# A two-layer graph network on one core: the order of the setup on VectorE, the schedule of the last blocks, and where the test's result is kept

## The chip, the core and the metric

The kernel runs on one core of a Trainium2 chip. The core has five engines with their own instruction streams: TensorE (PE; its weight loads are listed as PEld), VectorE (DVE), ScalarE (ACT), GpSimd (POOL) and SyncE (SP). DMAs are issued from the streams of SP and ACT, and gathers by index from POOL. The metric is the device time of one execution in microseconds (us), as the median of several. Beside it stands one profiled execution, whose span runs from the first to the last instruction.

## The reference

There are 12,500 nodes with 256 features each (`x`) and 200,000 edges (`src`, `dst`), sorted by `dst`. The draw makes `dst` go with the square of the edge's place: edge e of E points to about node 12500 (e/E)^2, so early nodes have many edges and late nodes few.

```python
def _sage_conv(x, src, dst, W_l, b_l, W_r):
    msgs = x[src]
    agg = jax.ops.segment_sum(msgs, dst, num_segments=N_NODES)
    deg = jax.ops.segment_sum(jnp.ones((src.shape[0],), x.dtype), dst, num_segments=N_NODES)
    mean = agg / jnp.maximum(deg, 1.0)[:, None]
    return mean @ W_l + b_l + x @ W_r
h = jax.nn.relu(_sage_conv(x, src, dst, W1_l, b1, W1_r))
h = jax.nn.relu(_sage_conv(h, src, dst, W2_l, b2, W2_r))
out = layernorm(x + h @ W3 + b3)
```

## The kernel before

**Two ways of summing.** Edges are cut into 1,563 tiles of 128, nodes into 98 blocks of 128. The first nodes, which have most edges, are summed as dense products: seven groups of 256 nodes, five of them in layer 1. For each group the kernel counts how many edges lead from every node to each of the 256 (`count`, L678 and below: comparisons `pick`, `low` and `aft` on DVE, products on PE, the result copied into `counts`), and then multiplies the table of all rows, split into three bf16 parts, with these counts (`product`, L667). Layer 2 uses the counts of layer 1 again: four are stored in DRAM and loaded, and one group is kept. The other nodes are summed by gathering: four indirect DMAs on POOL (L257) fetch 512 rows of a round into one of four buffers `got`; PE adds up 32 neighbouring nodes per tile (`part_ps`, L269), ACT copies the result (`some`), PE moves it to its place (`sum_ps`, L285), and DVE adds it to a ring of eight blocks, `sums` (L299).

**Blocks.** When a block's sums are complete, `first_block` (layer 1, in three pieces) or `last_block` (layer 2, in five) turns its own rows over on PE (L861), forms the products with the two weights (L884, L889), adds and applies the relu. The last layer turns h over again, forms the product with W3 (L956), and takes the layernorm on DVE and ACT. Layer 1 writes h to `h_d`, and its three parts to `h3_d`; both are read by layer 2, and a profile writes both as h_d.

**The order.** On PE and POOL the order is the program's own (`manual_schedule`, L445). The rounds of gathers set it: `layer` (L584) runs round after round, and in three parts of each round it places one piece of a waiting block, and as much of the counting and dense work (`dense`, a generator) as is due by then. The amount due grows evenly, from estimated costs, and reaches the whole 8 rounds before the last. A block waits in line from the round in which its sums are complete by the law of the draw: `at_least(t)` and `at_most(t)` bound the node that tile t begins with, by the square law moved by `SLACK` = 8 tiles. After the last round the rest of the dense generator is run out, and then the blocks that wait. The dense generator puts its two blocks in line only when it is run past its last product. With the amounts of this program, layer 2 reaches this point after the loop: blocks 6 and 7, of the last dense group, stand at the very end.

On DVE, ACT and SP a planner orders the instructions by its own simulated times and by the program's order as priority. Within an engine instructions then run in the order written, each waiting for its semaphores. A DMA of SP or ACT uses one of eight semaphores, and in the trace it waits until the DMA that used the semaphore before has landed.

**The setup.** `src` and `dst` are loaded as 13 x 128 x 128 integers by SP (`edges`, L304): `src_i`, `dst_i` and `nxt_i`, which is `dst` one edge on. ACT loads the first `dst` of tiles: of each tile by fours (`f4_i`, L333 and L337), by eights (`f8_i`, L340), of all early tiles (`f1_i`, L342), `fours_i` and `pair_i` (L343, L345). Indices are cast to floats, turned over on PE with the identity `ident` (L361), and written by DVE into tables (`columns`, L376): `src_t` (the gathers' indices), `lo_t` (an edge's place within its tile's 32 nodes), `lo2` (L433, a tile's place within 128). These are what the first gathers need. Behind them come the tables for counting (`low_t`, and `key_t` and `after_t` by group), with a round of gathers started between the groups (`early_round`), and then tests that the drawn edges obey the law and fit into the rooms (L497 to L544), each of which adds to a column of `bad`. The memory of the setup is then reused: ACT blanks the two `counts` there (L574).

**The result of the tests.** After layer 2, PE sums `bad`, DVE reduces it to one flag, and SP writes it to DRAM (L988), reads it back into the chip (L41), and every engine loads it into a register and branches over `by_sorting`, a slower version that fits any edges.

Of the kernel before, what the change touches and what calls it, by code (L numbers as in the profile page):

```python
# [23 lines left out]
P = 128  # L24
# [3 lines left out]
def kernel(tc, x, src, dst, w1l, b1, w1r, w2l, b2, w2r, w3, b3, out):  # L28

    args = (x, src, dst, w1l, b1, w1r, w2l, b2, w2r, w3, b3, out)
    flag = tc.nc.dram_tensor("unfit_d", (1, 1), I32).ap()
    by_runs(tc, *args, flag)
    with tc.tile_pool(name="flag", bufs=1) as pool:
        unfit_i = pool.tile([1, 1], I32, name="unfit_i")  # L40
        tc.nc.sync.dma_start(unfit_i, flag)  # L41
        unfit = tc.nc.values_load(
            unfit_i[0:1, 0:1], min_val=0, max_val=1,
            skip_runtime_bounds_check_because="it is clamped to 0..1 where it is made")
    with tc.If(unfit > 0):
        by_sorting(tc, *args)
# [3 lines left out]
def by_runs(  # L50
# [36 lines left out]
    FAR = 1 << 20  # L87
    SLACK = 8
    RB = 8
    RN = RB * P  # L90
    assert D % P == 0 and E % 2 == 0 and G * W == P


    def at_least(t):
        return N * (max(t - SLACK, 0) / NT) ** 2 - 2

    def at_most(t):
        return N * ((t + SLACK) / NT) ** 2 + 2

# [201 lines left out]
    with tc.tile_pool(name="setup", bufs=1) as su, \  # L301
            tc.tile_pool(name="setup_ps", bufs=2, space=PSUM) as su_ps:
        def edges(a, first, name, fill):
# [14 lines left out]
            return t  # L318

        src_i = edges(src, 0, "src_i", 0)  # L320
        dst_i = edges(dst, 0, "dst_i", FAR)
# [9 lines left out]
        whole = (NT // G) * G  # L331
        with nc.allow_non_contiguous_dma(reason="one edge of each tile"):
            nc.scalar.dma_start(f4_i[:, :NT // G], dst[0:whole * P].rearrange(  # L333
                "(g j l) -> j g l", j=G, l=P)[:, :, 0])
            if NT > whole:
                left = NT - whole
                nc.scalar.dma_start(  # L337
                    f4_i[0:left, NT // G:NG],
                    dst[whole * P:whole * P + (left - 1) * P + 1:P][:, None])
            nc.scalar.dma_start(f8_i, dst[lows[HG1] * P:PAIRS * P].rearrange(  # L340
                "(g j l) -> j g l", j=G, l=2 * P)[:, :, 0])
            nc.scalar.dma_start(f1_i, dst[None, 0:HC * P * P:P])  # L342
            nc.scalar.dma_start(fours_i, dst[0:P * P:P * G][:, None, None].to_broadcast([P // G, G, 1]))  # L343
            for c in range(C0, PAIRS // P):
                nc.scalar.dma_start(pair_i[:, c:c + 1], dst[c * P * P:(c + 1) * P * P:2 * P][  # L345
                    :, None, None].to_broadcast([P // 2, 2, 1]))

# [15 lines left out]
        nc.vector.tensor_copy(lanes_5[:, :, :LW // 5], steps_f[:, :LW].rearrange("p (a b) -> p a b", a=5))  # L363
        nc.vector.tensor_copy(steps_7[:, :, :NB // 7], steps_f[:, :NB].rearrange("p (a b) -> p a b", a=7))


# [65 lines left out]
        nc.vector.tensor_copy(within_f, within)  # L432
        nc.vector.tensor_scalar(lo2, after, within_f, None, op0=OP.add)  # L433

        for g in got:

            nc.vector.memset(g[:, :, D:D + 1], 1.0)
        nc.vector.memset(sums, 0.0)
        nc.vector.memset(degs, 0.0)
        nc.vector.memset(ones, 1.0)  # L440
        nc.vector.memset(ones_b, 1.0)
        nc.vector.memset(zeros_b, 0.0)

# [13 lines left out]

        nc.vector.tensor_copy(steps, steps_f)
        bits = su.tile([P, HC, P], I32, name="bits")
        low = su.tile([P, HC, P], F32, name="low")  # L460
        nc.vector.tensor_scalar(bits, src_i[:, :HC], P - 1, None, op0=OP.bitwise_and)
        nc.vector.tensor_copy(low, bits)
# [4 lines left out]
        start = su.tile([P, HC], F32, name="start")  # L467
        nc.vector.tensor_copy(start[:, 0:1], fours_i)
        nc.vector.tensor_copy(start[:, 1:], first[:, 1:HC])
        f1 = su.tile([1, HC * P], F32, name="f1")  # L470
        nc.vector.tensor_copy(f1, f1_i)
        off_f = su.tile([1, HC * P], F32, name="off_f")
        nxt_first = su.tile([P, HC], F32, name="nxt_first")
        nc.vector.tensor_copy(nxt_first, nxt_i[:, :HC, P - 1])
        most_c = max(b - a for a, b in spans)
# [20 lines left out]
        nxt_f = su.tile([P, CH, P], F32, name="nxt_f")  # L496
        nc.vector.tensor_copy(nxt_f, nxt_i)  # L497
        nc.vector.scalar_tensor_tensor(scr, dst_f, 0.0, nxt_f, op0=OP.add, op1=OP.is_gt,
# [10 lines left out]
        for sign in (-1, 1):  # L509
            law = su.tile([1, NG], F32, name="law", bufs=2)  # L510
            nc.vector.tensor_scalar(law, fours, float(G) / NT, float(sign * SLACK) / NT,
                                    op0=OP.mult, op1=OP.add)
            nc.vector.tensor_scalar(law, law, 0.0, None, op0=OP.max)
            nc.vector.tensor_tensor(law, law, law, op=OP.mult)
            scr4 = su.tile([1, NG], F32, name="scr4", bufs=2)
            nc.vector.tensor_scalar(scr4, f4[0:1], -float(sign), None, op0=OP.add)
            nc.vector.scalar_tensor_tensor(scr4, law, float(N), scr4, op0=OP.mult,
                                           op1=OP.is_gt if sign < 0 else OP.is_lt,
                                           accum_out=test(1))
# [63 lines left out]

    def layer(gathers, block, n_pieces, dense, dense_cost):  # L584

# [35 lines left out]
        for i in range(i0, n + 1):  # L621
            before = gathers.step()
            due = dense_cost * min(1.0, (i + 1 - i0) / (n - i0 - 8))
            for part in range(3):
# [12 lines left out]
    def exact(t, s, rest):  # L637
# [4 lines left out]

        nc.vector.tensor_tensor(rest, t, upper(t), op=OP.subtract)
        nc.vector.tensor_tensor(s[:, 2], rest, upper(rest), op=OP.subtract)
        nc.scalar.copy(s[:, 0], upper(t))
        nc.scalar.copy(s[:, 1], upper(rest))

    def split_rows(b):
        t = load_rows(x, N, b, "split_sb")
        s = work.tile([P, 3, D], BF16, name="parts")  # L650
        exact(t, s, work.tile([P, D], F32, name="rest", tag="own"))
        nc.sync.dma_start(x3_d[:, b], s)
# [320 lines left out]
    with tc.tile_pool(name="count_ps", bufs=2, space=PSUM) as count_pool:  # L973
        layer(gathers_1, first_block, 3, staged(stages_1), cost_of(stages_1))
    block_pool = ctx.enter_context(tc.tile_pool(name="block_ps", bufs=2, space=PSUM))
    count_pool = ctx.enter_context(tc.tile_pool(name="count_ps", bufs=1, space=PSUM))
    w2l_sb, w2r_sb = weight(w2l, "w2l_sb", "wl", nc.sync), weight(w2r, "w2r_sb", "wr", nc.sync)
    layer(Gathers(h_d, True), last_block, 5, staged(stages_2), cost_of(stages_2))


    with tc.tile_pool(name="result", bufs=1) as su:
# [6 lines left out]
        nc.sync.dma_start(flag, unfit)  # L988

# [368 lines left out]
```

## Time and profile before

| | us |
|---|---|
| median of three runs | 2829.16 |
| the three runs | 2829.16, 2819.84, 2829.44 |
| profiled execution, in all | 2817.42 |
| its span | 2815.6 |
| mean granted TensorE clock | 0.928 |
| first gather starts | 26.85 |
| last DVE work of the setup ends | 95.7 |
| last gather of layer 1, first of layer 2 | 1475.51, 1501.29 |
| last gather starts | 2759.22 |
| last product on PE ends | 2799.9 |

Lines of the profile give a start or a total in us, then the engine, the line of the program, the operation, what it writes and reads, its shape, how often it ran, and in brackets how long the engine had been idle before it and what ended that. SPq and ACTq are the moments in which SP and ACT issue a DMA. A group's "idle before" with "issue" is time in which the engine waited for nothing that the profile shows. Digits are left out of tiles' names, so f_i stands for f1_i, f4_i and f8_i, lo for lo2, and h_d for both tables.

### The profile page before, as it was taken

How to read it: one execution, taken by the hardware profiler on the slowest of the kernel's cores; microseconds unless marked ns; L12 is line 12 of the kernel's file. 1: busy time of each engine (PE TensorE's matmuls, PEld its weight loads, DVE VectorE, ACT ScalarE, POOL GpSimd, SP SyncE). 2: the span in 40 equal slices, each digit the busy share in tenths (PEclk: the TensorE clock that was granted, in tenths of full speed). 3: DMA queues.
4: the chain of work that ended last, by engine and by line, in shares of the span. 5: the costliest groups of instructions: out<-in, count | busy, mean ns of one | idle time of the engine just before them, and what ended most of it. 6: DMA issues, size and time to landing. Idle time of an engine off the chain costs nothing. (4 is left out here: it accounts for less than half of the span.)

```text
span 2815.6 us, 54531 instructions
## 1 busy us (share of the span) xinstructions
PE 2321.8 (82%) x18268; PEld 1594.5 (57%) x18268; DVE 1525.3 (54%) x5362; ACT 1098.5 (39%) x2270; POOL 2014.5 (72%) x2074
## 2 busy tenths in 40 slices
PE   3466668988988999999985787778788889999995
PEld 1122225656656766767753565556566666677773
DVE  5688886755655676676662134443233344444443
ACT  0433675655554565565551123342111122222222
POOL 5767677777777777777775777777777767777771
PEclk9977778999989999999999999999899999999997
DMA  4467679869859879868855777777889889888872
GB/s 115 137 202 221 191 219 306 265 193 315 272 183 329 268 234 305 266 194 268 263 167 167 233 249 223 225 228 251 273 282 302 286 282 303 284 264 271 270 241 65
DMA packets 420983, 676.56 MB, mean 240 GB/s; under 512 B 72419, under 2 KB 279385, under 8 KB 420697
## 3 DMA queue, kind: packets, MB, share of 16 engines
q1 hardware_dynamic: 316807, 401.13, 43.7%
q0 software_dynamic: 99072, 270.66, 31.2%
q8 instruction: 150, 2.46, 0.4%
q10 hardware_dynamic: 4818, 1.19, 0.3%
q14 instruction: 136, 1.11, 0.1%
HBM read 582.84 MB, written 89.92 MB: 239 GB/s over the span
## 5 line engine op out<-in xcount | busy, mean ns | idle before, releaser
L257 POOL DMA_INDIRECT got<-in_x_dram,src_t x1076 | 1072.4, 997 | 401.3 <-issue 281.5
L257 POOL DMA_INDIRECT got<-h_d,src_t x988 | 940.0, 951 | 343.7 <-issue 258.7
L667 PE MATMUL dense_ps<-counts,rows 128*128 128x256 bf16 x7056 | 954.0, 278 | 93.6 <-DMA rows<-h_d 53.2
L667 PEld LDWEIGHTS <-rows 128*128 128x128 bf16 x7056 | 671.2, 99 | 316.9 <-issue 84.2
L735 ACT CAST counts<-count_ps 128x686 f32 (+2 forms) x620 | 539.8, 871 | 246.7 <-PE count_ps L729 188.0
L269 PE MATMUL part_ps<-got,one 128*32 128x257 f32 (+1 forms) x4128 | 362.8, 425 | 161.7 <-DMA got<-h_d,src_t 107.6
L729 PE MATMUL count_ps<-pick,low 128*128 128x490 bf16 (+2 forms) x1052 | 320.8, 358 | 57.7 <-DVE low L694 32.0
L691 DVE TENSOR_SCALAR pick<-steps,key_t 128x686 bf16<-128x686 f16 (+2 forms) x748 | 301.1, 405 | 57.6 <-PE count_ps L729 43.0
L213 DVE TENSOR_TENSOR one<-lo_t,lane_b 128x128 f32<-128x128 bf16 x516 | 147.3, 285 | 313.7 <-PE part_ps L269 310.4
L279 ACT COPY some<-part_ps 128x257 f32<-128x257 f32 (+1 forms) x361 | 134.3, 372 | 421.6 <-PE part_ps L269 420.8
L694 DVE TENSOR_SCALAR low<-lanes,low_t 128x130 bf16<-128x130 f16 x748 | 201.7, 271 | 93.7 <-PE count_ps L733 91.9
L269 PEld LDWEIGHTS part_ps<-got,one 128*32 128x32 f32 x4128 | 86.9, 112 | 275.5 <-issue 219.9
L285 PE MATMUL sum_ps<-two,some 128*128 128x128 f32 x1444 | 239.9, 292 | 2.0 <-DVE sums L299 1.9
L892 ACT COPY sums<-zero 128x256 f32<-128x256 f32 x172 | 69.4, 403 | 412.1 <-PE block_ps L889 410.2
L299 DVE TENSOR_TENSOR sums<-sums,sum_ps 128x256 f32 x361 | 148.3, 411 | 145.4 <-PE sum_ps L285 112.7
L285 PEld LDWEIGHTS sum_ps<-two,some 128*128 128x128 f32 x1444 | 208.7, 204 | 16.6 <-issue 9.1
L729 PEld LDWEIGHTS <-low 128*128 128x128 bf16 x1052 | 104.3, 100 | 159.4 <-DVE low L694 61.5
L895 DVE TENSOR_TENSOR own<-block_ps,biases 128x256 f32<-128x256 f32 x196 | 82.7, 422 | 191.7 <-PE block_ps L889 188.4
L863 ACT COPY own_t<-block_ps 128x256 f32<-128x256 f32 x294 | 108.9, 372 | 128.4 <-PE block_ps L861 127.2
L699 DVE TENSOR_SCALAR aft<-steps,after_t 128x98 bf16<-128x98 f16 x621 | 155.9, 251 | 0.0
L898 ACT ACTIVATE h<-own 128x256 f32<-128x256 f32 x196 | 81.6, 416 | 149.6 <-DVE own L896 146.7
L733 PE MATMUL count_ps<-aft,low 128*128 128x98 bf16 x614 | 133.7, 218 | 0.0
(179 smaller groups left out, 2454.6 us busy)
## 6 DMA issues: line engine op xcount, KB each, us to landing
rows<-h_d SPq DMA_DIRECT2D x343, 384.0 KB
rows<-x_d SPq DMA_DIRECT2D x245, 384.0 KB
count_d<-counts SPq DMA_DIRECT2D x28, 896.0 KB
counts<-count_d SPq DMA_DIRECT2D x28, 896.0 KB
x_sb<-in_x_dram SPq DMA_DIRECT2D x194, 128.0 KB
x_d<-parts SPq DMA_DIRECT2D x98, 192.0 KB
h_d<-parts SPq DMA_DIRECT2D x98, 192.0 KB
got<-in_x_dram,src_t POOLq DMA_INDIRECT x1076
```

Of the source, the lines that this page charges most:

```text
L213: nc.vector.tensor_tensor(one, lo[:, a:a + n * (G - 1) + 1:n].unsqueeze(2).to_broadcast([P, G, W]), lane_b[:, :W].unsqueeze(1).to_broadcas ...
L257: rows = nc.gpsimd.indirect_dma_start(out=g[:, j, :D], out_offset=None, in_=self.table, in_offset=bass.IndirectOffsetOnAxis(ap=src_t[:, e: ...
L269: strip = nc.tensor.matmul(part_ps[j * W:(j + 1) * W, :width], lhsT=one[:, j], rhs=g[:, j, :width], start=r == 0, stop=r == n - 1)
L279: nc.scalar.copy(some[:, :width], part_ps[:, :width])
L285: nc.tensor.matmul(sum_ps[:, c], lhsT=some[:, c * P:(c + 1) * P], rhs=two, start=True, stop=True)
L299: nc.vector.tensor_add(own, own, sum_ps[:, :NC])
L667: nc.tensor.matmul(ps[:, c], lhsT=rows[:, b % 2, k, c * P:(c + 1) * P], rhs=c_sb[:, b, :DN], start=False, stop=b == NB - 1 and k == 2 and ...
L691: nc.vector.tensor_scalar(r[:, :w * NB], steps[:, :w * NB], key_t[g][:, t - lo_g:t - lo_g + 1], None, op0=OP.is_equal)
L694: nc.vector.tensor_scalar(low.rearrange("p (a b) -> p a b", a=5), lanes_5[:, :, :LW // 5], low_t[:, t:t + 1], None, op0=OP.is_equal)
L699: nc.vector.tensor_scalar(aft.rearrange("p (a b) -> p a b", a=7), steps_7[:, :, :NB // 7], after_t[g][:, t - lo_g:t - lo_g + 1], None, op0 ...
L729: nc.tensor.matmul(c[:, a * NB:b * NB], lhsT=s, rhs=r[:, a * NB:b * NB], start=True, stop=alone)
L735: nc.scalar.copy(to[:, :, bass.ds(off_act.at(t), w)], c.rearrange("p (d s) -> p s d", s=NB))
```

## The change

Five things change.

- In the setup, DVE is put under the program's order from the first load to `lo2`. The memsets of gather buffers, sums and constants move up, behind the first constants. The six `pair_i` loads move from the end of ACT's loads to their head.
- What comes behind `lo2` on DVE and does not need it in any case gets a dependency on it (`later`): the first instructions of counting, of the tests, and of the first three blocks of split rows.
- The slack of the law is 8 tiles up to tile NT - 65, then 5, and 3 for the last 16. The test of the law (L511) runs over three ranges for each sign, and so has four more instructions.
- `layer` takes the number of rounds by which the dense work ends ahead of the last round, 8 for layer 1 and 14 for layer 2. From there on everything that is left of it is due at once, its last step included.
- The flag is a tile on the chip that lives through the whole program. It is computed between the layers instead of behind layer 2, and neither written to DRAM nor read back.

```diff
-    flag = tc.nc.dram_tensor("unfit_d", (1, 1), I32).ap()
-    by_runs(tc, *args, flag)
     with tc.tile_pool(name="flag", bufs=1) as pool:
-        unfit_i = pool.tile([1, 1], I32, name="unfit_i")
-        tc.nc.sync.dma_start(unfit_i, flag)
+        flag = pool.tile([1, 1], I32, name="flag")
+        by_runs(tc, *args, flag)
         unfit = tc.nc.values_load(
-            unfit_i[0:1, 0:1], min_val=0, max_val=1,
+            flag[0:1, 0:1], min_val=0, max_val=1,
...
-    SLACK = 8
+    SLACKS = [(0, 8), (NT - 64, 5), (NT - 16, 3)]
+    def slack(t):
+        return [by for since, by in SLACKS if since <= t][-1]
     def at_least(t):
-        return N * (max(t - SLACK, 0) / NT) ** 2 - 2
+        return N * (max(t - slack(t), 0) / NT) ** 2 - 2
...
+        in_order = ExitStack()
+        in_order.enter_context(tc.manual_schedule(engines={DVE}))
         src_i = edges(src, 0, "src_i", 0)
...
+            for c in range(C0, PAIRS // P):
+                nc.scalar.dma_start(pair_i[:, c:c + 1], dst[c * P * P:(c + 1) * P * P:2 * P][
+                    :, None, None].to_broadcast([P // 2, 2, 1]))
             nc.scalar.dma_start(f4_i[:, :NT // G], dst[0:whole * P].rearrange(
...
-            for c in range(C0, PAIRS // P):
-                nc.scalar.dma_start(pair_i[:, c:c + 1], dst[c * P * P:(c + 1) * P * P:2 * P][
-                    :, None, None].to_broadcast([P // 2, 2, 1]))
...
+        for g in got:
+            nc.vector.memset(g[:, :, D:D + 1], 1.0)
+        nc.vector.memset(sums, 0.0)
+        nc.vector.memset(degs, 0.0)
+        nc.vector.memset(ones, 1.0)
+        nc.vector.memset(ones_b, 1.0)
+        nc.vector.memset(zeros_b, 0.0)
...
-        nc.vector.tensor_scalar(lo2, after, within_f, None, op0=OP.add)
-        for g in got:
-            nc.vector.memset(g[:, :, D:D + 1], 1.0)
-        nc.vector.memset(sums, 0.0)
...
+        first_tables = nc.vector.tensor_scalar(lo2, after, within_f, None, op0=OP.add)
+        in_order.close()
+        def later(op):
+            tc.add_manual_dep(op.ins, first_tables.ins.name, LANDED, reason="the first gathers' tables")
...
-        nc.vector.tensor_copy(steps, steps_f)
+        later(nc.vector.tensor_copy(steps, steps_f))
...
-        nc.vector.tensor_scalar(bits, src_i[:, :HC], P - 1, None, op0=OP.bitwise_and)
+        later(nc.vector.tensor_scalar(bits, src_i[:, :HC], P - 1, None, op0=OP.bitwise_and))
...
-            nc.vector.tensor_scalar(law, fours, float(G) / NT, float(sign * SLACK) / NT,
-                                    op0=OP.mult, op1=OP.add)
+            for since, by in SLACKS:
+                c = -(-since // G)
+                later(nc.vector.tensor_scalar(law[:, c:], fours[:, c:], float(G) / NT,
+                                              float(sign * by) / NT, op0=OP.mult, op1=OP.add))
...
-    def layer(gathers, block, n_pieces, dense, dense_cost):
+    def layer(gathers, block, n_pieces, dense, dense_cost, left):
...
-            due = dense_cost * min(1.0, (i + 1 - i0) / (n - i0 - 8))
+            due = dense_cost * (i + 1 - i0) / (n - i0 - left) if i + 1 < n - left else 1e8
...
-        exact(t, s, work.tile([P, D], F32, name="rest", tag="own"))
+        leaves = exact(t, s, work.tile([P, D], F32, name="rest", tag="own"))
+        if b < 3:
+            later(leaves)
...
-        layer(gathers_1, first_block, 3, staged(stages_1), cost_of(stages_1))
+        layer(gathers_1, first_block, 3, staged(stages_1), cost_of(stages_1), 8)
...
-    layer(Gathers(h_d, True), last_block, 5, staged(stages_2), cost_of(stages_2))
...
-        unfit = su.tile([1, 1], I32, name="unfit")
-        nc.vector.tensor_scalar(unfit, n_bad, 1.0, None, op0=OP.min)
-        nc.sync.dma_start(flag, unfit)
+        nc.vector.tensor_scalar(flag, n_bad, 1.0, None, op0=OP.min)
+    layer(Gathers(h_d, True), last_block, 5, staged(stages_2), cost_of(stages_2), 14)
```

`later` also stands around the casts of `fours_i`, `f1_i`, `nxt_i` (its last edges and the whole).

More of the change, by code (lines that the diff above doesn't have):

```diff
@@ L91, in by_runs @@
     assert D % P == 0 and E % 2 == 0 and G * W == P
+    def slack(t):
+        return [by for since, by in SLACKS if since <= t][-1]
     def at_least(t):
-        return N * (max(t - SLACK, 0) / NT) ** 2 - 2
+        return N * (max(t - slack(t), 0) / NT) ** 2 - 2
     def at_most(t):
-        return N * ((t + SLACK) / NT) ** 2 + 2
+        return N * ((t + slack(t)) / NT) ** 2 + 2
     HG1, HG, DN = 5, 7, 256
@@ L432, in by_runs @@
         nc.vector.tensor_copy(within_f, within)
-        nc.vector.tensor_scalar(lo2, after, within_f, None, op0=OP.add)
-        for g in got:
-            nc.vector.memset(g[:, :, D:D + 1], 1.0)
-        nc.vector.memset(sums, 0.0)
[L439 to L442, printed above, removed]
+        first_tables = nc.vector.tensor_scalar(lo2, after, within_f, None, op0=OP.add)
+        in_order.close()
+        def later(op):
+            tc.add_manual_dep(op.ins, first_tables.ins.name, LANDED, reason="the first gathers' tables")
         ctx.enter_context(tc.manual_schedule(engines={PE, POOL}))
@@ L467, in by_runs @@
         start = su.tile([P, HC], F32, name="start")
-        nc.vector.tensor_copy(start[:, 0:1], fours_i)
+        later(nc.vector.tensor_copy(start[:, 0:1], fours_i))
         nc.vector.tensor_copy(start[:, 1:], first[:, 1:HC])
         f1 = su.tile([1, HC * P], F32, name="f1")
-        nc.vector.tensor_copy(f1, f1_i)
+        later(nc.vector.tensor_copy(f1, f1_i))
         off_f = su.tile([1, HC * P], F32, name="off_f")
         nxt_first = su.tile([P, HC], F32, name="nxt_first")
-        nc.vector.tensor_copy(nxt_first, nxt_i[:, :HC, P - 1])
+        later(nc.vector.tensor_copy(nxt_first, nxt_i[:, :HC, P - 1]))
         most_c = max(b - a for a, b in spans)
@@ L496, in by_runs @@
         nxt_f = su.tile([P, CH, P], F32, name="nxt_f")
-        nc.vector.tensor_copy(nxt_f, nxt_i)
+        later(nc.vector.tensor_copy(nxt_f, nxt_i))
         nc.vector.scalar_tensor_tensor(scr, dst_f, 0.0, nxt_f, op0=OP.add, op1=OP.is_gt,
@@ L641, in upper @@
             return a.bitcast(BF16).rearrange("p (n h) -> p n h", h=2)[:, :, 1]
-        nc.vector.tensor_tensor(rest, t, upper(t), op=OP.subtract)
+        leaves = nc.vector.tensor_tensor(rest, t, upper(t), op=OP.subtract)
         nc.vector.tensor_tensor(s[:, 2], rest, upper(rest), op=OP.subtract)
@@ L646, in exact @@
         nc.scalar.copy(s[:, 1], upper(rest))
+        return leaves
     def split_rows(b):
```

## The prediction

> **What bounds the kernel now.** I read the busy shares first, then the largest groups, then who held up the gathers, and last three stretches in order of time: the start, the end, and the busiest part of layer 2. First the engines, then the gathers' two groups (busy time, mean of one, idle before them).
>
> ```profile
> PE 2321.8 (82%) x18268; PEld 1594.5 (57%) x18268; DVE 1525.3 (54%) x5362; ACT 1098.5 (39%) x2270; POOL 2014.5 (72%) x2074
> ```
>
> ```profile
> L257 POOL DMA_INDIRECT got<-in_x_dram,src_t x1076 | 1072.4, 997 | 401.3 <-issue 281.5
> L257 POOL DMA_INDIRECT got<-h_d,src_t x988 | 940.0, 951 | 343.7 <-issue 258.7
> ```
>
> PE has the larger share, but POOL sets the pace: an undisturbed gather takes 0.95 us and 0.30 us to issue, so 2064 of them need 2064 x 1.25 = 2580 of the span's 2815.6 us. What POOL waited for (us, times, longest):
>
> ```profile
> POOL got L257 <- issue: 540.1, 1772, 0.6
> POOL got L257 <- PE part_ps L269: 84.5, 69, 9.7
> POOL got L257 <- DMA h_d<-parts: 24.8, 1, 24.8
> POOL got L257 <- DVE src_t L376: 24.1, 1, 24.1
> ```
>
> Besides its own issue, POOL loses 84.5 us to PE in small pieces, 24.8 us once between the layers, and 24.1 us at the start. After its last gather (2760.2) another 55 us pass. So three places can shorten the run: before the first gather, between the layers, behind the last gather. A microsecond saved before the first gather moves all later rounds with it, as long as PE keeps up.
>
> **The setup: about 13 us.** DVE in the order of time, before the change (start, duration, instruction, idle before it):
>
> ```profile
> 10.22 0.83 DVE L382 CAST src_f<-src_i 128x1280 f32<-128x1280 int32 x1 [4.20 <-DMA src_i<-in_src_dram]
> 17.99 0.35 DVE L409 CAST f<-f_i 4x391 f32<-4x391 int32 x1 [6.95 <-DMA f_i<-in_dst_dram]
> ...
> 19.21 0.20 DVE L361 TENSOR_SCALAR ident<-diff 128x128 f32<-128x128 int32 x1
> ...
> 23.99 0.17 DVE L390 CAST begin<-pair_i 128x6 f32<-128x6 int32 x1 [4.44 <-DMA w1l_sb<-in_L_gnn_W_l_dram]
> ...
> 25.88 1.28 DVE L376 TENSOR_SCALAR src_t<-src_ps 128x512 int32<-128x512 f32 x2
> ...
> 36.91 0.40 DVE L433 TENSOR_SCALAR lo<-after,within_f 128x186 f32<-128x186 f32 x1
> ```
>
> The sources are ready as floats at 11.05, but DVE then stands 6.95 us before f4 and 4.44 us before the pairs, with ident (which every transpose needs) and the first eviction of src_t queued behind. The first gather starts at 26.85. In program order ident, lanes and the memsets (sums 1.98, degs 1.02, the rest small) are done by about 8 us, below src's landing. From 11.05: four transposes at 1.97/8 = 0.25 us, 1.0; one eviction, 1.28/2 = 0.64; 0.3 to issue: the first gather starts at about 13, some 14 us sooner.
>
> The rest must follow, or the four gather buffers run full. Four rounds of gathers take 16 x 1.3 = 21 us, so the first part_ps is wanted by 34. On ACT's queue the six pair loads now go first, f4, its rest, f8, f1 and fours behind them. Before, the six took 7.85 us from first to last, most of it waiting for earlier landings; six issues alone are 6 x 0.6 = 3.6. On SP's queue dst_i was issued at 9.12, 6.5 us late behind src_i's landing. I let dst_i land at about 13 (before: 18.8) and f4 and f8 by 19. Then dst_f 1.0, first and begin 0.6, rel 1.5, scr 0.8 and 1.5, transposes and three evictions 3, lo2's part 1.3, the small f4 and f8 work with its two matmuls 5: first tables at about 27, against 37.3. From that 10 comes off what now stands behind them but was done before: steps, two bits, low, high, 0.60 + 0.42 + 0.48 + 0.47 + 0.49 = 2.5 us. DVE was idle for 17 of the 58 us between the tables and the last test (95.6), waiting for gathers that now also come 14 us sooner; 41.5 busy + 2.5 + four more law pieces, 1 us, fit into the stretch. So the end of setup, and with it ACT's 22 us of blanking the counts (95.76 to 117.77) and the first counting, come about 14 us sooner. The stretch 118 to 180, where POOL loses 20 us because counting sets the pace (DVE busy 51.4 of 62), keeps its length and moves too.
>
> A rule that speaks against this: the Trainium skill, "SBUF — State Buffer", section "SBUF: two separate sides", says that a VectorE instruction in a two-port mode shuts GpSimd out and stops the descriptors of its DMAs. Early gathers now lie beside more setup casts. The row: gathers 1 to 40 took 57.2 us instead of 40 x 1.25 = 50, so 7 us are lost already, single gathers 2.36 and 2.67 us. By the row alone nothing is added, since the same instructions meet other gathers; by the rule up to 9 casts and evictions of some 0.8 us, 7 us more, meet gathers that once came after them. I take 1 us, near the row. Setup: 13; ends 7 (dst_i or f8 land where they did) and 17.
>
> **Between the layers: 3 us.** The order of blocks follows from the slack: with 5 and then 3 tiles in place of 8, blocks 88 to 95 become ready one round sooner. In layer 1 block 95's products (L884 and L889, 3.55 us at 1487.04) now stand ahead of the last sum_ps instead of behind it. The two dense blocks of layer 1 were already done seven rounds earlier, so nothing else moves. The last h still waits for deg_d's round trip, 1486.93 to 1494, in which SP held two loads behind an x_sb load until 1490.84; that block's transposes come about 5 us sooner, the row's own landing does not. Between 1 and 5, I take 3. The test's matmul and its two DVE instructions (0.21, 0.15, 0.12) go into this gap and cost nothing; without the gap 0.5.
>
> **Behind the last gather: 16.5 us.** PE's last 40 us:
>
> ```profile
> 2763.38 1.08 PE L269 MATMUL part_ps<-got,one 128*32 128x256 f32 x8 [1.25 <-DMA got<-h_d,src_t]
> ...
> 2772.27 1.06 PE L285 MATMUL sum_ps<-two,some 128*128 128x128 f32 x4
> ...
> 2787.65 1.03 PE L884 MATMUL block_ps<-w2l_sb,d_sb 128*128 128x256 f32 x4
> ...
> 2793.01 1.03 PE L884 MATMUL block_ps<-w2l_sb,d_sb 128*128 128x256 f32 x4
> ...
> 2797.80 2.08 PE L956 MATMUL block_ps<-w_sb,own_t 128*128 128x256 f32 x4 [0.52 <-ACT own_t L863]
> ```
>
> Products of d_sb are blocks 6 and 7 of the last dense group. Its last dense product ends at 2736.6 and d_sb is copied at once, but in PE's written order these blocks are queued only after the loop. Now all dense work is forced out 14 rounds before the end, and blocks 6 and 7 run in rounds 232 to 237, where the four dense steps of a round (4 x 0.83 = 3.3 us) are gone. After the last sum there remain: block 95's transpose and final product; two transposes; the products of 96 and 97 (2 x 2.0); two transposes; two final products. With DVE and ACT between (0.42 + 0.48 + 0.42 + 0.37 and waits) that is 13 us, against 2799.9 - 2772.3 = 27.6. The last sum itself comes 2 us sooner, block 94's products being out of the last round. 14.5 + 2 = 16.5, between 13 and 19.
>
> **The result on chip: 1 us.** SP's last issues:
>
> ```profile
> 2800.94 0.24 SPq L988 DMA_DIRECT2D unfit_d<-unfit  x1
> 2802.15 0.33 SPq L969 DMA_DIRECT2D out_dram<-z  x1
> 2802.95 0.24 SPq L41 DMA_DIRECT2D unfit_i<-unfit_d  x1
> ```
>
> [...] In the trace they landed after 1.09 and 1.12 us, and out's landing (2803.66) comes only 0.4 us before the flag's (2804.07); every engine waited for both before it branched. So by the row 0.4, plus 0.5 for a register load that may come earlier. If the engines no longer wait for out before they branch, the 3.6 us of PE's branch and POOL's 4.15 us drain run ahead, up to 5. I take 1.
>
> **What it costs: 3 us.** In layer 2 the dense work is spread over 233 rounds instead of 239, 2.6% more in each. The busy part (stretch, length, busy time by engine, clock, DMA share, GB/s):
>
> ```profile
> 2400.00:2736.00 336.00, 318.98 (x2570) 243.14 (x2570) 155.39 (x468) 82.98 (x233) 252.80 (x266) 0.99 0.83 268
> ```
>
> POOL is full here (266 x 1.25 = 332), PE at 95%; 2.6% of its dense half is some 4 us, into 17 idle. From 2000 to 2400 PE waits for rows at a DMA share of 0.88 and POOL loses 16 us; 2.6% of that stretch's dense time, 400 x 0.6 x 0.026, is 6. Between 0 and 10, I take 3.
>
> Sum: 13 + 3 + 16.5 + 1 - 3 = 30.5. The profiled execution took 2817.4 us in all (span 2815.6 and 1.8 around it) and would take 2787. It is one of four times of this program, 2817.4, 2819.8, 2829.2 and 2829.4; I subtract from their mean, 2824, and get 2793.5, rounded 2794.
>
> **The rivals.** (1) The early gathers outrun their tables: f8 and f4 land late behind the pairs, or the DVE chain of keys sets the pace. Against it: 17 us of idle DVE. Setup then gives 0 to 2: gain 18, 2806. (2) PE or the row loads bound all of layer 2: then dense work ends no sooner in time, and six rounds are added behind it, 6 x 5 = 30 us, so 2821. For it: rows waits of 46.9 us between 2000 and 2736; against: 1501 to 2000, where PE is busy 77%. (3) Slower: SP, DVE and ACT of the rest are ordered by a planner from its own timing, and a changed start reorders them. The place is SP's queue in layer 2, where a row load stands behind an x_sb load that waits for its buffer, as the deg loads did at 1490.84. It must cost 30.5 us to cancel the gain, and 44 to be slower by 0.5%: rows waits would have to double, 0.13 us on each of 343 loads; then 2840. (4) That the fallback runs: excluded, since the drawn dst stay within 8 nodes of the law over the last 64 tiles, and three tiles there are 48 nodes.
>
> **How the numbers follow.** The forecast 0.68 (2782 to 2806 alone), rival 1 0.15, rival 2 0.10, rival 3 0.07. 0.5% is 14 us, about what a measurement here can tell from no change: below 2815 is faster. Faster 0.66 + 0.13 + 0.03 = 0.82; same 0.02 + 0.02 + 0.07 = 0.11; slower 0.07. Leaving out rival 3 and most of rival 2 above, and a tail below, gives 2779 to 2815.
>
> **What would show it.** First gather near 13 and lo2 near 27 in the timeline; counts blanked from about 82; POOL's wait for h_d near 22; no d_sb products behind the last gather, and 39 us instead of 55 from it to the end; POOL's waits on part_ps in layer 2 up by no more than 10. Wrong it is if first tables come after 35, or if rows waits grow by tens of us.

## The result and the profile after

The changed kernel takes 2788.66 us (median of four, 2780.44 to 2801.16) beside 2829.06 us for the kernel before (four, 2819.84 to 2829.44). The ratio is 0.9873, with a 95% interval from 0.9841 to 0.9905: 36 us faster, between 27 and 45. Measured again later on another chip it was 0.9851 (0.9820 to 0.9883). The forecast of 2794 lies 5 us from the median. Its parts did not all come out as written, and errors of opposite sign stand behind the agreement.

The profiled execution took 2801.16 us (span 2799.4) and is the slowest of its four. The two profiles therefore differ by only 16 us, and one place in layer 2, shown under "The places over ten profiles", has a share in that. First, what POOL waited for (us in all, times, longest):

```profile
POOL got L259 <- issue: 540.7, 1773, 0.6
POOL got L259 <- PE part_ps L271: 110.1, 80, 7.8
POOL got L259 <- DMA h_d<-parts: 24.4, 1, 24.4
...
POOL got L259 <- DVE src_t L390: 8.5, 1, 8.5
```

The wait at the start fell from 24.1 to 8.5 us. The wait between the layers hardly moved (24.8 to 24.4), and waits on part_ps rose from 84.5 to 110.1. Part of the rise is seen in the setup, another in layer 2 (below). POOL's first gather, and DVE in the order of time:

```profile
11.32 1.10 POOL L259 DMA_INDIRECT got<-in_x_dram,src_t  x1 [8.53 <-DVE src_t L390]
```

```profile
4.01 0.21 DVE L366 TENSOR_SCALAR ident<-diff 128x128 f32<-128x128 int32 x1
...
8.39 0.75 DVE L396 CAST src_f<-src_i 128x1280 f32<-128x1280 int32 x1
...
10.35 0.69 DVE L390 TENSOR_SCALAR src_t<-src_ps 128x512 int32<-128x512 f32 x1 [1.21 <-PE src_ps L387]
...
22.54 1.03 DVE L400 CAST dst_f<-dst_i 128x1664 f32<-128x1664 int32 x1 [10.29 <-DMA dst_i<-in_dst_dram]
...
36.11 0.41 DVE L447 TENSOR_SCALAR lo<-after,within_f 128x186 f32<-128x186 f32 x1 [1.35 <-PE after L442]
```

The identity is ready at 4.2 and the first gather starts at 11.32, against 26.85 before. But then DVE, now bound to the program's order, stands idle for 10.29 us in front of dst_f, and lo2 ends at 36.5, no earlier than before (37.3). SP's queue shows why:

```profile
6.17 0.40 SPq L311 DMA_DIRECT2D dst_i<-in_dst_dram  x1
6.94 0.38 SPq L315 DMA_DIRECT2D dst_i<-in_dst_dram  x1
17.64 0.22 SPq L319 DMA_DIRECT2D dst_i<-in_dst_dram  x1
17.91 0.39 SPq L311 DMA_DIRECT2D nxt_i<-in_dst_dram  x1
```

`edges` loads dst_i in three pieces. The two large ones landed by 15.2. The third, one row of 64 integers (L319), was not issued before 17.64: its semaphore was the one that ACT's load of f4 had used, and in the trace f4's last piece landed at 17.63. The small load landed at 22.52, 4.9 us after its issue, and dst_f followed. The profile of before has the same late third piece:

```profile
17.54 0.22 SPq L317 DMA_DIRECT2D dst_i<-in_dst_dram  x1
```

There the DMA that had used its semaphore was the first piece of dst_i itself, which landed at 17.52; the third landed at 18.77. Still the end of the setup came sooner, as ACT's blanking of the counts shows, first before and then after the change:

```profile
95.76 22.01 ACT L574 COPY counts<-zero 128x13034 f32<-128x13034 f32 x2 [8.25 <-DVE scr L544]
```

```profile
84.84 22.01 ACT L587 COPY counts<-zero 128x13034 f32<-128x13034 f32 x2 [3.04 <-DVE scr L557]
```

The end of PE's work:

```profile
2773.07 0.64 PE L271 MATMUL part_ps<-got,one 128*32 128x256 f32 x8
...
2778.17 0.61 PE L287 MATMUL sum_ps<-two,some 128*128 128x128 f32 x4
...
2783.23 1.03 PE L901 MATMUL block_ps<-w2l_sb,sums 128*128 128x256 f32 x4
...
2788.68 1.89 PE L973 MATMUL block_ps<-w_sb,own_t 128*128 128x256 f32 x8
```

No product of d_sb is left here; the last one starts at 2729.5. From the last sum to the last product 12 us pass, where it was 28. SP's only late issues are those of the output:

```profile
2792.19 1.01 SPq L986 DMA_DIRECT2D out_dram<-z  x2
```

The flag is no longer written and read back, and the engines do not come to the branch together any more. In the kernel before all five loaded the flag between 2804.4 and 2804.6. Here PE loads it at 2789.36, while its last products still run, and branches for 3.87 us; ACT loads it at 2791.91, DVE at 2792.43, SP at 2793.25; and POOL's drain of 4.15 us is over by 2775.84, where before it ran from 2810.63 to 2814.78.

### The profile page after: what moved, and what is told of

Read it like the earlier page. It is cut to its first block, busy times and chain, and to the rows that moved or that the text cites. A ratio compares the mean times of both kernels' runs of the same rounds, so it can differ in the third digit from the quotient of the medians.

```text
span 2799.4 us, 54469 instructions
## 1 busy us (share of the span) xinstructions
PE 2322.7 (83%) x18268; PEld 1595.9 (57%) x18268; DVE 1526.5 (55%) x5366; ACT 1099.7 (39%) x2270; POOL 2018.4 (72%) x2074
## 4 chain that ended last, share of the span: by engine, by line
PE 44%; DMA 24%; POOL 12%; issue 8%; DVE 7%; ACT 3%; DVEq 1%; SPq 0%; ACTq 0%; POOLq 0%
PE dense_ps L684 16%; POOL got L259 12%; PE part_ps L271 6%; DMA got<-h_d,src_t 5%; DMA rows<-x_d 5%; PE block_ps L901 5%; PE count_ps L746 4%; PE block_ps L906 4%; DMA rows<-h_d 4%; PE sum_ps L287 4%; DMA x_sb<-in_x_dram 3%; DMA got<-in_x_dram,src_t 2%; PE block_ps L973 2%; DMA x_d<-parts 2%; PE block_ps L878 2%
```

## The experiments

Twelve runs were made, in three groups. The kernel before ran beside each group on the same chip. In the first group that chip was slower: the kernel before took 3318.63 us there. The gathers themselves took as long as elsewhere, but POOL waited far more for PE. In the changed kernel on this chip (us in all, times, longest):

```profile
POOL got L259 <- PE part_ps L271: 288.4, 124, 11.9
POOL got L259 <- remote: 170.9, 103, 3.2
```

"Remote" is a releaser that the trace does not show. So of this group I use the ratios and what happens before the first gather and behind the last. PE's products took no longer there (the median dense product 0.27 us on both chips); what delayed the releases stays open.

**The whole change again (e4, e9).** No edit.

> The changed kernel once more, for a second profile and more times. Theory: the difference to before is near 35 us, the first gather starts near 11 and lo2 ends near 36 again; what the gathers lost between 640 and 880 of layer 1 in the first profile of it is variation between executions and comes out otherwise here. Rival: the loss of about 12 us in these rounds is the change's own and stands here too.

On the slower chip the ratio was 0.9900 (0.9862 to 0.9937), 33 us of 3319. The first gather came at 11.33 again.

> The changed kernel again, beside the runs that follow. Theory: 34 to 40 us faster than before (ratio 0.986 to 0.988); by places 10 before gather 256, 2 between the layers, 16 from the last gather to the last product, 7 from there to the end, less some 4 in layer 2. On a chip of the slower pace the ratio is near 0.99 and the last two places stay.

On a chip on which the kernel before takes 2826.24, the ratio was 0.9851 (0.9820 to 0.9883): 42 us, 33 to 51. The stretch from gather 640 to gather 880, in which the first two profiles differed by 12 us (315.9 and 327.8), took 319.8 here and 323.9 in a second profile of the kernel before. It was a difference between executions, not of the change.

**The setup alone (e1, e11).** The kernel before, with the setup's part of the diff, a slack of 8 everywhere, dense work due as before, and the flag in DRAM:

```diff
+    SLACKS = [(0, 8)]
...
+        in_order.enter_context(tc.manual_schedule(engines={DVE}))
...
+            for c in range(C0, PAIRS // P):
+                nc.scalar.dma_start(pair_i[:, c:c + 1], dst[c * P * P:(c + 1) * P * P:2 * P][
...
+        first_tables = nc.vector.tensor_scalar(lo2, after, within_f, None, op0=OP.add)
+        in_order.close()
```

> The kernel before with the setup's part of the change alone (DVE in program order up to lo2, memsets and pair loads first, what does not need lo2 behind it); slack 8 everywhere, dense work due as before, flag through DRAM. Theory: the gain is made before the first gather (about 15 us there), the late tables (lo2 near 36) give back part of it by the end of the setup, and the rest moves all later rounds: 8 to 12 us faster than before. Rival: the early gathers outrun their tables and the key chain and counting set the pace behind it, so that the gain is gone by the end of layer 1: 0 to 3 us. Third: without the other parts the end of the program pays nothing, so the last gather must start sooner by just what the total gains.

Ratio 0.9979 (0.9956 to 1.0002) on the slower chip, 7 us and no verdict. The last gather started at 3241.92, beside 3251.57 and 3254.65 in the two kernels of that chip with the old setup, 10 to 13 us sooner. So it ran again:

> The kernel before with the setup's part alone, again, on the chip of the runs beside it. Theory: 8 to 12 us faster than before, as at gather 256. Rival: the gain is gone by the end of layer 1: 0 to 4.

Ratio 0.9959 (0.9935 to 0.9982): 11.6 us, 5 to 18. The rival's end, no gain, is excluded.

**The end of the dense work alone (e2, e12).**

```diff
-            due = dense_cost * min(1.0, (i + 1 - i0) / (n - i0 - 8))
+            due = dense_cost * (i + 1 - i0) / (n - i0 - left) if i + 1 < n - left else 1e8
...
+    layer(Gathers(h_d, True), last_block, 5, staged(stages_2), cost_of(stages_2), 14)
```

> The kernel before with the dense work's end alone changed (14 rounds ahead of the last round in layer 2, its last step included; layer 1 stays at 8). Theory: the products of blocks 6 and 7 leave the stretch behind the last gather, from it to the last product some 24 to 26 us in place of 41, and the denser rounds of layer 2 give back 3 to 5: 11 to 14 us faster. Rival: the denser rounds make PE set the pace of layer 2 and give it all back, 0 to 4 us.

Ratio 0.9971 (0.9948 to 0.9994) there. From the last gather to the last product 36.6 us passed, beside 47.4 and 44.2 in the two other kernels of that chip that keep the old end. The absolute 24 to 26 did not hold at that pace.

> The kernel before with the end of the dense work alone, again, on the same chip. Theory: 14 to 16 us less from the last gather to the last product, 0 to 6 of them given back in layer 2: 9 to 15 us faster. Rival: given back wholly, 0 to 4.

Ratio 0.9959 (0.9933 to 0.9985): 11.6 us, 4 to 19. From the last gather to the last product 25.3 us, against 40.8 and 42.1 in the profiles of the kernel before. So 16 us are gained there and, by the time, about 4 are given back; with the interval of the time, anything from 12 to nothing. The trace of this run shows where, below.

**The flag alone (e3).**

```diff
-        unfit_i = pool.tile([1, 1], I32, name="unfit_i")
-        tc.nc.sync.dma_start(unfit_i, flag)
+        flag = pool.tile([1, 1], I32, name="flag")
+        by_runs(tc, *args, flag)
```

> The kernel before with the flag kept on chip and computed between the layers, nothing else. Theory: the engines' waits for the flag's landing go and they load it and branch while the last block is still under way, so that from the last product to the end 9 us pass in place of 16: 6 to 7 us faster. Rival (the forecast's row): only the two landings count, 0.4 to 1 us.

In time 0.9984 (0.9957 to 1.0011), which settles nothing. The trace does. PE's last products and SP's issue of the output, of a span of 3304.2 us:

```profile
3294.42 1.34 PE L954 MATMUL block_ps<-w_sb,own_t 128*128 128x256 f32 x4 [0.52 <-ACT own_t L861]
...
3298.38 0.33 SPq L967 DMA_DIRECT2D out_dram<-z  x1
```

From the last product to the end 8.5 us pass, and 15.6 and 15.7 in the two kernels beside it that keep the flag in DRAM. Over all fourteen profiles of this study this stretch is 15.6 to 15.8 with the flag in DRAM and 8.2 to 8.8 with it on chip, on every chip. In the mean the stretch is 7.2 us shorter, and not 0.4 to 1.

**The kernel before again (e5).** No edit.

> The kernel before once more, for a profile beside the other runs. Theory: first gather near 27, lo2 near 37, some 40 us from the last gather to the last product and 15 from there to the end, whatever the chip's pace; the pace of the gathers between differs from chip to chip and from execution to execution.

First gather at 26.27, lo2 done at 36.7, 42.1 us from the last gather to the last product, 15.7 from there to the end. Gather 1075 came 14.5 us later than in the first profile of the same kernel, and layer 2 took 6.6 us less. That is the size of what one profile can't resolve in the middle of the run.

**The small load off SP's queue (e6, e10).** The changed kernel, with the one-row piece issued by POOL:

```diff
-                nc.sync.dma_start(t[rows:rows + 1, CH - 1, :rest], a[None, E - rest:E])
+                nc.gpsimd.dma_start(t[rows:rows + 1, CH - 1, :rest], a[None, E - rest:E])
```

> The changed kernel with the one-row rest of src, dst and nxt loaded from POOL's stream, so that it stands behind no other queue's loads. In the changed kernel's profile dst_i's rest waited on SP for f4's 1560 small pieces and landed at 22.5, and dst_f followed it. Theory: dst_f starts at 15 to 17, lo2 ends near 29 in place of 36.5, POOL's longest wait on part_ps at the start shrinks by as much, and gather 40 comes 4 to 7 us sooner; in all 3 to 6 us faster, which the times can hardly show. Rival: the chain of keys or f4's own landing holds lo2 at 34 or later, nothing gained.

DVE in the first of the two runs:

```profile
14.00 1.03 DVE L400 CAST dst_f<-dst_i 128x1664 f32<-128x1664 int32 x1 [1.29 <-DMA dst_i<-in_dst_dram]
...
29.23 0.41 DVE L447 TENSOR_SCALAR lo<-after,within_f 128x186 f32<-128x186 f32 x1 [1.34 <-PE after L442]
```

dst_f starts at 14.0 and lo2 ends at 29.6: the small load was what held the tables. Among gathers 16 to 40 POOL no longer waits (0.1 us in all beyond the usual 0.30 each, 5.8 in the changed kernel), and gather 40 starts at 72.27 instead of 78.62. The ratio was 0.9865 (0.9838 to 0.9891).

> The changed kernel with the one-row rests on POOL's stream, again, beside the changed kernel itself on the same chip. Theory: gather 40 comes 6 us sooner than in the changed kernel and gather 256 some 4; in time 2 to 6 us faster than it, ratio to before 0.0007 to 0.002 lower. Rival: the counting that follows sets the pace by gather 128 and nothing is left: equal times.

Beside the changed kernel on one chip: 0.9846 (0.9809 to 0.9882) against 0.9851. Gather 40 came 5.2 us sooner, gather 256 2.1 us, and in time the two are equal within the intervals. So the rival holds as far as can be measured, and the version was not shown to beat the changed kernel.

**Eight rounds in layer 2 (e7).** The changed kernel with the 8 of layer 1 in layer 2 too; the last step is still forced out:

```diff
-    layer(Gathers(h_d, True), last_block, 5, staged(stages_2), cost_of(stages_2), 14)
+    layer(Gathers(h_d, True), last_block, 5, staged(stages_2), cost_of(stages_2), 8)
```

> The changed kernel with layer 2's dense work forced out 8 rounds before the last, as in layer 1, instead of 14. Theory: forcing its last step out is what takes blocks 6 and 7 into the loop; eight rounds are enough for one of them and part of the other, so from the last gather to the last product pass 3 to 8 us more than with 14, and layer 2's gathers end 2 to 3 us sooner: 1 to 5 us slower. Rival: eight rounds hold both, and the evener spread wins: 2 to 3 us faster.

Ratio 0.9862 (0.9832 to 0.9891), the same as e6 beside it. From the last gather to the last product it took 28.4 us, some 3 more than with 14, and layer 2's gathers took 1248.7, the least of all. With 8 rounds and the last step forced out both blocks still ran ahead of the end (their products of d_sb start at 2722.28 and 2731.90, the last gather at 2751.04), so the forcing, not the 14, carries most of the gain. The changed kernel itself did not run on this chip, and by the time no run shows whether 14 rounds are any better than 8.

**Slack 8 throughout (e8).** The changed kernel with:

```diff
-    SLACKS = [(0, 8), (NT - 64, 5), (NT - 16, 3)]
+    SLACKS = [(0, 8)]
```

> The changed kernel with the law's slack at 8 tiles throughout. Theory: block 95's products go back behind the last sum of layer 1, 1 to 3 us more between the layers, and one more block piece stands behind the last gather, 0 to 3 us: 1 to 5 us slower. Rival (the first profile, where the wait between the layers shrank by 0.4 us only): the wait for deg_d's round trip sets the end of layer 1 and nothing changes there; 0 to 1 us.

Ratio 0.9884 (0.9856 to 0.9912), beside 0.9862 and 0.9865: some 6 us slower than its neighbours, with intervals that overlap. The neighbours, e6 and e7, each have another edit, and their profiles do without most of the loss in layer 2 that e8's has (table below), so the 6 us are not the slack's alone. Between the layers 27.5 us passed instead of 25.4. PE in this kernel, the last sum of layer 1 and block 95 behind it:

```profile
1488.35 0.68 PE L287 MATMUL sum_ps<-two,some 128*128 128x128 f32 x4 [0.89 <-DVE sums L301]
...
1490.26 2.05 PE L901 MATMUL block_ps<-w1l_sb,sums 128*128 128x256 f32 x4 [1.08 <-DVE sums L301]
```

and in the changed kernel, block 95 ahead of it:

```profile
1487.42 2.05 PE L901 MATMUL block_ps<-w1l_sb,sums 128*128 128x256 f32 x4 [1.67 <-DVE sums L301]
1489.26 1.77 PE L906 MATMUL block_ps<-w1r_sb,own_t 128*128 128x256 f32 x4
1490.86 0.61 PE L287 MATMUL sum_ps<-two,some 128*128 128x128 f32 x4
```

## The places over ten profiles

One profile of each kernel is too few. The table has all profiles from chips of the usual pace, by what each kernel has of the change (us; the runs with the small load on POOL are in brackets):

| stretch | without the part | with it | gain in the mean | forecast |
|---|---|---|---|---|
| start to gather 256 | 402.9, 407.8, 408.6 | 395.0, 396.9, 393.6, 397.1, 391.9 (390.3, 394.8) | 11.5 | 13 |
| last gather of layer 1 to first of layer 2 | 25.8, 26.8, 27.8, 27.5, 28.5 | 25.4, 24.8, 25.8 (23.0, 25.5) | 2.4 | 3 |
| first to last gather of layer 2 | 1257.9, 1251.3, 1251.8, 1248.7 | 1262.7, 1265.0, 1264.5, 1263.1 (1251.9, 1253.9) | -8 | -3 |
| last gather to last product | 40.8, 42.1, 40.3 | 23.8, 26.0, 26.8, 25.3 (26.0, 23.9) | 15.7 | 16.5 |
| last product to end | 15.6, 15.7, 15.7, 15.8 | 8.8, 8.7, 8.4, 8.2 (8.4, 8.6) | 7.2 | 1 |

The means of the first row leave the brackets out; those of the others have them in, and the loss in the third row is 11 without them. The fourth row leaves out e7 (28.4), which has 8 rounds and the last step forced. From gather 256 to the end of layer 1 the kernels with the new setup took 5.7 us more in the mean (1082.7 against 1077.0). Two executions of the kernel before alone differ by 10 there, and the setup alone gained 11.6 us in twelve timed runs, so I do not count this as a cost; the interval of that gain, 5 to 18, does not exclude it.

**The cost in layer 2 is in one place.** With 14 rounds the values fall into two clusters, near 1264 and near 1253. Gathers 1784 to 1824 make the difference: 50.4 to 51.2 us in the four kernels without the part, 60.7 to 63.1 in four with it, and 54.2 and 54.4 in the two in brackets. e12, which has the schedule alone, has the loss, and e7, which lacks only the 14 rounds, has not, so it belongs to these. In this stretch the last group's counts are loaded and the group before it becomes blocks. The timeline of e9 at this place:

```profile
2400.34 0.43 SPq L806 DMA_DIRECT2D counts<-count_d  x1
...
2407.68 0.33 SPq L872 DMA_DIRECT2D x_sb<-in_x_dram  x1
...
2410.60 0.64 PE L271 MATMUL part_ps<-got,one 128*32 128x256 f32 x8
...
2414.06 0.43 DVE L969 TENSOR_TENSOR x_sb<-x_sb,biases 128x256 f32<-128x256 f32 x1 [4.63 <-DMA x_sb<-in_x_dram]
...
2415.84 0.69 PE L878 MATMUL block_ps<-ident,h 128*128 128x128 f32 x2 [3.57 <-ACT h L915]
2416.32 1.48 PE L684 MATMUL dense_ps<-counts,rows 128*128 128x256 bf16 x6
...
2421.24 0.64 PE L271 MATMUL part_ps<-got,one 128*32 128x256 f32 x8
```

An x_sb load is issued behind a load of 896 KB of counts, while the DMA engines are full (share 1.07 by the profile's count from 2404 to 2412), and DVE can use it 6.4 us later. DVE adds the bias to it in its written order, so the next block's `own`, ACT's `h`, and PE's transposes of that h stand behind it, and with them every later product in PE's written order. PE is idle for 3.57 us and then slow: six dense products take 1.48 us where they take 0.82. The same place in e10:

```profile
2401.32 0.64 PE L271 MATMUL part_ps<-got,one 128*32 128x256 f32 x8
...
2404.25 0.43 DVE L969 TENSOR_TENSOR x_sb<-x_sb,biases 128x256 f32<-128x256 f32 x1 [4.11 <-DMA x_sb<-in_x_dram]
...
2406.03 0.44 PE L878 MATMUL block_ps<-ident,h 128*128 128x128 f32 x2 [3.05 <-ACT h L915]
2406.31 0.82 PE L684 MATMUL dense_ps<-counts,rows 128*128 128x256 bf16 x6
...
2409.89 0.64 PE L271 MATMUL part_ps<-got,one 128*32 128x256 f32 x8
```

The same chain, with a wait 0.5 us shorter; and the products run on at full speed. From one part_ps to the next it takes 8.6 us instead of 10.6. Two windows just behind these waits give the granted clock (the columns are the stretch, its length, busy time and instructions of PE, PEld, DVE, ACT and POOL, then clock, DMA share and GB/s). In e9:

```profile
2416.00:2420.00 4.00, 4.00 (x18) 3.40 (x19) 0.68 (x2) 0.70 (x3) 0.62 (x1) 0.61 0.42 138
```

and in e10:

```profile
2406.00:2410.00 4.00, 3.97 (x30) 3.34 (x34) 1.30 (x4) 0.89 (x3) 3.08 (x4) 1.00 0.66 217
```

The clock is 0.61 in one and 1.00 in the other, and the products go with it: over the whole of e9 a dense product takes 0.42 us at half the clock and 0.27 at the full one. The Trainium skill, "TensorE: Matmul & The Clock Gate", section "Part 1: The HAM clock gate", says that after an idle window of about 3.4 us TensorE falls to half its clock and needs as long a busy window to come back. The pair of 3.57 and 3.05 seems to fit, but the traces do not show such a limit. In the ten profiles of the table, from 200 us on, I counted PE's waits that began after 3 us at the full clock, and those behind which the mean clock was under 0.75 in at least one of the next four microseconds: 54 of 317 waits of 1.0 to 1.5 us, 264 of 371 of 2.0 to 3.4 us, and 141 of 144 of 3.4 us and more. So e10's full clock behind 3.05 us is the rarer case. The 10.6 us here were two longer than the 8.6 there, of which 0.5 is the wait; the rest came with the lower clock, and which wait brings that on is not settled by its length alone.

Each of the four profiles with the loss has a second such wait for h some 35 us later, of 2.33 to 3.28 us, with the lower clock behind it; e6 and e10 wait 1.34 and 1.60 us there and keep the full clock, although e6's first wait was 4.07 and was followed by the low clock. In all POOL loses 10.7 to 13.0 us in this stretch in the four, 3.9 and 4.4 in e6 and e10, and 0.2 to 1.2 in the kernels without the part. Why the second wait is shorter in the two in brackets was not settled, and no run moved the x_sb load to test the chain. Nor can it be said which of the unprofiled executions have the loss. The profiled executions of e9 and of the changed kernel's first group took 2808.80 and 2801.16, the other executions of the same two groups 2783.9 and 2785.9 in the mean, so most of them may well not have it.

## Why the prediction held, step by step

**Setup, 13: right in size, wrong on the way.** "First gather near 13" was 11.3. "I let dst_i land at about 13" is the step that failed, and with it "first tables at about 27": they came at 36.5. I had counted SP's issues and not that a small load waits for the DMA that used its semaphore before, here one of another queue. The third piece's late issue stood in the profile of before, at 17.54, and I did not read it. By the sign that I had set ("Wrong it is if first tables come after 35") the setup's argument was wrong; the sum held all the same. By gather 40 the gain of 15.3 us had fallen to 6.4: 4.9 went into waits on part_ps, and 3.9 into longer gathers (11.8 us beyond 0.95 each, against 7.9). Then most of it came back: at gather 64 it was 10.3, at 128 7.1, at 256 11.5. The counts were blanked from 84.8, 10.9 us sooner ("from about 82"), and between gathers 128 and 256 POOL waited 5.4 us less. The gain at gather 256 goes with the start of that blanking: in e10 it came 1.8 us sooner than in e9 (82.83 and 84.64) and gather 256 2.1 us, although gather 40 came 5.2 us sooner. So waits at the start seem to use up time that counting takes from POOL later anyway; this is a reading of these numbers and was not tested by itself. Rival 1, that the gain is lost when the tables come late, had its condition and not its consequence.

**The rule on the shared port** (the Trainium skill, "SBUF — State Buffer", section "SBUF: two separate sides", as the setup's step has it). I took 1 us by the row and named 7 by the rule. Gathers 0 to 40 took 3.9 us more and gathers 40 to 64 2.0 less, as they would if the setup's instructions met other gathers. The net is 2, nearer to the row; that the longer gathers come from the port was not shown.

**Between the layers, 3: right** in the table (2.4, or 2.0 without the brackets). In the first two profiles it was 0.4, and there alone it would have looked wrong.

**Behind the last gather, 16.5: right,** 15.7, by the mechanism named: no d_sb products, the four dense steps of those rounds gone. What I had not seen is that forcing the last step out does most of it (e7).

**The result on chip, 1: the term that was mis-sized,** 7.2. The text had named the mechanism, that PE's branch and POOL's drain run ahead once the engines don't wait for the output, and put it at "up to 5". I took the landing row because it stood in the profile (and read it as 0.4; out's last part landed at 2803.84, 0.2 us ahead of the flag), and let the alternative go for lack of a row. What left the path can be read from SP, which ends it after the change (6.8 us in the first two profiles). Its branch came 4.9 us behind the last product before and 3.5 after, as the flag's landing is gone: 1.4 us. From its branch to the end 10.7 us passed before and 5.3 after: 5.4 us, as POOL's drain of 4.15 us, with 1.2 us of another POOL instruction ahead of it, no longer stands there. A branch itself is not gained. PE's of 3.6 us runs ahead, but SP too goes on only 3.7 us after its branch before and 3.1 after. So POOL's drain, which stood in the trace of before, was the row to read.

**Denser dense, -3: by the trace -8 in profiled runs, by the time about -4** (15.7 less the 11.6 of e12, whose interval is 4 to 19), and not for the reason given. Density cost nothing that can be seen: the two runs in brackets are within 1.5 us of the mean of the kernels with 8 rounds. By the trace the loss is the mechanism of rival 3, a written order of SP and DVE in which a load of x_sb comes late, at one place and worth 10 to 12 us. It never came near the 44 us at which it would have decided.

Together the measured terms make 11.5 + 2.4 + 15.7 + 7.2 - 4 = 33, against 30.5 forecast, and 36 (27 to 45) and 42 (33 to 51) measured for the whole. The flag's 6 us too little made up for the rest, and that is luck. So is part of the nearness of forecast and median, 5 us: the 30.5 were taken from 2824, the mean of four times, and from the median of 2829.06 they would have led to 2798.6, 10 us off. From the last gather's end to the end of the span 32 us passed in the first profile, where 39 had been forecast; the flag's term is the difference. Rivals 2 and 3 are excluded as outcomes, and rival 1 by e11.

## What to carry to other kernels

Ahead of an end in which all engines meet, read the chain from the last product to the last instruction as one path, engine by engine: what only one engine does there while the others wait (here POOL's drain) is gained when the meeting goes, and what the last engine must do itself (here SP's register load and branch) stays. In a setup, follow the last and smallest piece of every load to its semaphore; a row of 64 integers held the tables for 7 us. And compare places, not totals: one profile of each kernel gave 16 us, and only the ten together and the times showed which steps had held.

## What the hardware showed unexpectedly

PE's branch at the end takes 3.4 to 3.9 us in all fourteen profiles, where those of the other engines are recorded with 0.04 to 0.08. But ACT, DVE and SP start their next instruction only 2.5 to 4.6 us after their branch in all fourteen, so the pause is not PE's alone; what fills it the traces do not show. A wait of PE of 2.0 to 3.4 us mostly costs more than itself: behind 264 of 371 the clock was lower, and the dense products of the next four microseconds took 0.38 us in the mean there and 0.27 behind the others. And one chip ran the same program 17% slower (3318.63 against some 2827 us) with gathers and dense products of the same length, while POOL waited 288.4 instead of 110.1 us for part_ps; the cause stays open.
